# Block products for P4 in layer 0, gate sums moved to POOL and ScalarE, attention read from PSUM

## The chip, the cores and the metric

The kernel runs on one core of a Trainium2 chip. The metric is the device time of one execution in microseconds, taken as the median of several runs. A profiled execution, with every instruction's start and end, is read beside it. The engines are named as in the profile: PE is TensorE's matmul, PEld its weight load, DVE is VectorE, ACT is ScalarE, POOL is GpSimd, and SP is SyncE, which issues most DMAs.

## The reference

128 graphs of 128 nodes with 512 features go through two layers of attention with 8 heads of 64. Everything is float32.

```python
# layer 0, for each graph
Q, K, V = x @ W_q + b_q, x @ W_k + b_k, x @ W_v + b_v
scores = Q K^T / sqrt(64)                       # per head
scores += a[:, None] + c[None, :] + b_g + log(adj + 1e-9)   # a = x @ w_g[:512], c = x @ w_g[512:]
x = softmax(scores) V + x
# layer 1
q, k, v = x @ Wq.T + bq, x @ Wk.T + bk, x @ Wv.T + bv
logits = q k^T / sqrt(64) + log(clip(adj, 1e-8))
out = softmax(logits) v @ Wo.T + bo
x = layer_norm(x + out) * gamma + beta
```

## The kernel before

Four graphs make a tile. There are 64 tiles in a row: tiles 0 to 31 are layer 0 and tiles 32 to 63 are layer 1, and each layer 1 tile reads what the layer 0 tile of the same graphs stored in DRAM (`X1D`). A tile has three matrix products of 512x512 (V, Q, K), and a layer 1 tile a fourth (O), which is taken for the tile before, so that its attention has time to finish. The last tile has its own path.

Each matrix is Strassen-Winograd: seven products of half the size, P1 to P7, instead of eight. A whole product is eight matmuls of 256 columns (sixteen records in the trace) that accumulate in one PSUM bank. Bank `a` (tags p0 and p3, alternating by matrix) takes P1, then P6 and P7 on top of it, each copied out by ACT (t1, u2, u3) before the next is added, and at last P4. Bank `b` (p2) takes P5 and then P3. DVE adds the copies to the banks to get the four output blocks: C11 from P2 and t1, C22 from P5 and u3, C12 from P3 and u2, C21 from bank `a` after P4. A product named in `inside` is itself done by seven products of a quarter of the size ("block products", function `inner` inside `matrix`): four phases, and after each DVE accumulates a block of the bank into t1 (P2) or u3 (P4) and adds parts of it to the output. Before the change `INSIDE` holds P2 for tiles 1 to 63 and P4 for tiles 33 to 63 only; the Q and K of tile 32 and the O of tile 32 have neither. POOL makes the sums of operands: `sums` the four T tiles, `inner_sums` the sums for a block product, and `Strassen.combine_inner` the sums of the weights.

The order is written out by hand. A matrix has seven slots, and the list `row_` says which product goes to which slot (`SLOTS`, and `phases` for the four phases of P2). P4's phases come in slots 0, 2, 3 and 4 of the next matrix. Everything else is put ahead of a slot (`pre`) or behind it (`post`) with `put`, counted from the tile's first slot (`first`) or from the first slot after its K (`a`). `InOrder` makes every engine keep the program's order, so an instruction that waits holds up all that stands behind it on its engine.

Attention of a tile runs while the next tile's matrices are computed. `scores` makes K Q^T of four graphs, in the order of `graphs`: the first, second and fourth go to PSUM buffers of tag s (two of them, two banks each), the third to p1 and the free one of p0 and p3 (`spare`). ACT takes exp from PSUM to SBUF; in layer 0 the gate's c is its bias. `weigh` multiplies by the transposed adjacency on DVE. `mix` multiplies by V, which has a column of ones for the sums, into two more buffers of tag s; ACT copies them to SBUF (`OR`), and `normalise` divides on DVE. In layer 0 it also adds x on POOL and stores the tile. In layer 1 `move` transposes blocks by 16 DMAs for each pair of graphs, and `turn` transposes inside the blocks on DVE.

In layer 0 `gate` multiplies a graph's x by one half of w_g and sums it, in one DVE instruction, eight times in a tile. `add_row` adds the V bias to x on POOL. `count` keeps a record of whether the softmax sums were in range.

Of the kernel before, what the change touches and what calls it, by code (L numbers as in the profile page):

```python
# [134 lines left out]
def fast_path(ctx, tc, args, GOOD, bad):  # L135
# [38 lines left out]
    INSIDE = {t: ("P2", "P4") if t > NG else ("P2",) if t else () for t in range(LAST)}  # L174
# [78 lines left out]
    def gate(t, b, s):  # L253

        if (b, s) == (0, 0):
            C[t] = small.tile([P, 2, G], F32, tag="c", name=f"c_{t}", bufs=2)
        nc.vector.scalar_tensor_tensor(
            GW[:, 2], XN[t, b // 2][:, b % 2], 1.0, GW[:, s], op0=ALU.mult, op1=ALU.mult,
            accum_out=C[t][:, s, b : b + 1],
        )  # L260
# [37 lines left out]
    def matrix(n, name, W, Bs, side, out_tile, dst, bias=None, inside=("P2",)):  # L298
# [60 lines left out]
        def unit(i):  # L359
            i, *phase = i.split(".")  # L360
            if phase:
                if i in inside:
                    return inner(i, *phase)
                if (i, *phase) == ("P2", "1"):
                    t["c"] = bank("p1")
                    product("P2", t["W"], t["B"], t["c"], side, True)
                    add(0, 0, t["c"], t["t1"])
                return
            if i == "P4" and i in inside:
                return  # L370
            if i == "C22":
                return add(1, 1, t["b"], t["u3"])
            if i == "P1":
                t["W"], t["B"] = W(), Bs()
                out_tile()
                t["a"] = bank("p3" if n % 2 else "p0")
            elif i == "P5":
                t["b"] = bank("p2")
            p = t["b" if i in ("P5", "P3") else "a"]
            product(i, t["W"], t["B"], p, side, i in ("P1", "P5"))  # L380
            if i == "P1":
                kept("t1", p, 0, 2)
            elif i == "P6":
                kept("u2", p, None, 1)
            elif i == "P7":
                kept("u3", p, 1, 1)
            elif i == "P4":
                for _, _, o in dst(1, 0, 0, 4):
                    copy(o, p, 1)
            elif i == "P3":  # L390
                if bias is None:
                    add(0, 1, p, t["u2"])
                else:
                    for _, _, o in dst(0, 1, 0, 4):
                        for h, b in biased(0):
                            nc.vector.scalar_tensor_tensor(o[:, h], p[:, h], b, t["u2"][:, h], op0=ALU.add, op1=ALU.add)
# [43 lines left out]
    E = {}  # L440

    def scores(t, graphs, spare=None):
# [4 lines left out]
        for i, b in enumerate(graphs):  # L447
# [20 lines left out]
            if i != 2:  # L468
                pieces = [(e, s[b][2].rearrange("p r c j -> p (r c) j"))]
            for e, p in pieces:  # L470
                nc.scalar.activation(
                    e, p, AF.Exp, scale=SCALE, **({"bias": C[t][:, 1, b : b + 1]} if L == 0 else {})
                )

    def weigh(t, b):
        e = E[t, b]
        nc.vector.tensor_tensor(e, e, AD[t][:, b : b + 1].to_broadcast([P, H, N]), ALU.mult)

    def mix(t, graphs):


        a = {}
        for b in graphs:
            if b % 2 == 0:
                OR[t, b // 2] = work.tile([P, 2, H, HD + 1], F32, tag="o", name=f"o_{t}_{b // 2}", bufs=2)
            a[b] = ps.tile([P, 2, D], F32, tag="s", name=f"av_{t}_{b}", bufs=2)
            for h in range(H):
                for half in HALVES:
                    i = (h % KC) * (HD + 1)
                    nc.tensor.matmul(  # L490
                        a[b][half, h // KC, i : i + HD + 1], E[t, b][:, (h % 2) * KC + h // 2, half], V[t][:, b // 2, h // KC, b % 2 * KC + h % KC],
                        start=True, stop=True,
                    )
        for b, p in a.items():
            nc.scalar.copy(
                OR[t, b // 2][:, b % 2].rearrange("p (s c) d -> p s (c d)", s=2), p[:, :, 0 : KC * (HD + 1)]
            )

    def normalise(t, k):

        L, g = split(t)
        o = OR[t, k]
        if t not in RC:
            RC[t] = small.tile([P, G, 2, KC], F32, tag="rc", name=f"rc_{t}", bufs=2)
        rc = RC[t][:, 2 * k : 2 * k + 2].rearrange("p b s c -> p b (s c)")
        sums_ = o[:, :, :, HD]
        if L == 0:
            ga = GATE[t][:, 2 * k : 2 * k + 2].rearrange("p (b o) -> p b o", o=1).to_broadcast([P, 2, H])
            gated = small.tile([P, 2, H], F32, tag="gated", name=f"gated_{t}_{k}")
            nc.vector.tensor_tensor(gated, sums_, ga, ALU.mult)  # L510
            nc.vector.reciprocal(rc, gated)
            norm = small.tile([P, 2, H], F32, tag="norm", name=f"norm_{t}_{k}")
            nc.vector.tensor_tensor(norm, rc, ga, ALU.mult)
        else:
            nc.vector.reciprocal(rc, sums_)
            norm = rc
        v = o[:, :, :, 0:HD]
        nc.vector.tensor_tensor(
            v, v, norm.rearrange("p b (h o) -> p b h o", o=1).to_broadcast([P, 2, H, HD]), ALU.mult
        )  # L520
        if L == 0:
            xn = XN[t, k]
            for b in range(2):
                xb = xn[:, b].rearrange("p (h d) -> p h d", d=HD)
                nc.gpsimd.tensor_tensor(xb, v[:, b], xb, ALU.add)
            nc.sync.dma_start(X1D[g][2 * k : 2 * k + 2].rearrange("b p d -> p b d"), xn)
# [8 lines left out]
    def move(t, k, engines):  # L535
# [4 lines left out]
        v = OR[t, k].rearrange("p b (c r) d -> p (b c) r d", r=2)  # L540
# [144 lines left out]
    for (which, t), n in at.items():  # L685
        if t < NG:
            phases = EARLY if t == 0 else dict(v=(3, 4, 5, 7), q=(1, 2, 3, 5), k=EARLY)[which]
        elif t == NG or (which, t) == ("v", NG + 1):
            phases = dict(v=(3, 4, 5, 7), q=(1,), k=(0,), o=EARLY)[which]
# [4 lines left out]
        if (which, t) == ("o", NG):  # L694
            phases = (0,)
        for i, slot_ in enumerate(phases):
            row_[7 * n + slot_].append((mats[n], f"P2.{i + 1}"))
        row_[7 * n + 5].append((mats[n], "C22"))

# [9 lines left out]
    for t in range(LAST):  # L709
# [4 lines left out]
        if t + 1 < LAST:  # L714
            visit, weighed, mixed, graphs = (
                (3, (3, 3, 4, 5), (5, 7), (0, 1, 2, 3)), (3, (3, 3, 4, 5), (5, 7), (0, 1, 2, 3)), (5, (5, 5, 5, 7), (7, 9), (2, 3, 0, 1)),
# [4 lines left out]
            for i in range(2):  # L721
                m, k = a + mixed[i], graphs[2 * i] // 2
                put(pre, m, mix, t, (2 * k, 2 * k + 1))
                put(post, m + ((1, 4), (1, 0))[L][i], normalise, t, k)
                if L == 1:
                    put(post, m + (3, 1)[i], move, t, k, [nc.sync, nc.gpsimd] if t == NG and i else [nc.sync])
        if t + 1 < LAST:
            put(post, a + 16, count, t)

        n, late = t + 1, int(t > NG)  # L730
        if n < LAST:
            put(post, first + (2 if t else -1), load_tiles, n)
            for b in range(G):
                put(post, first + (-1 if t == 0 else 2 + (8 if t > NG + 1 else 11) * (b // 2) * late), load_graph, n, b, nc.sync)
                put(post, first + ((8, 9, 16, 16), (19, 20, 23, 24))[late][b], lambda n, b: turn(XT[n][:, b]), n, b)
            put(post, first + (11, 16 if t == NG + 1 else 14)[late], load_adjacency, n, nc.sync)
            put(post, first + (17, 31 if t > NG else 26)[late], turn_adjacency, n)
            put(post, first + (13, 17)[late], lambda n: TS.update({n: quarters(XT[n])}), n)
            put(post, first + (17, 20)[late], lambda n: inner_sums(TS[n], n), n)
            for s in Strassen.SUMS:  # L740
                put(post, first + (18, 24)[late], lambda n, s: sums(TS[n], n, s), n, s)
            if "P4" in INSIDE[n]:
                put(post, first + (18, 24)[late], lambda n: inner_sums(TS[n], n, "P4"), n)
        if L == 0:
            if g + 1 < NG:
                put(post, first + 17, load_natural, t + 1)
            for k, i in enumerate((1, 7, 10, 11, 13, 14, 18, 20)):
                put(post, first + i, gate, t, k // 2, k % 2)
            put(post, first + 21, gate_exp, t)
            for k in range(2):  # L750
                put(post, first + (11, 25)[k], add_row, t, k)
        else:
            put(post, first + (16 if t == NG + 1 else 12), load_natural, t)
            for k in range(2):
                put(post, first + ((27, 28) if t == NG else (28, 29) if t == LAST - 1 else (28, 32))[k], add_row, t, k)
            if n < LAST:
                f = slot("v", n, 0)
                first_pair, turned = (f + 17, f + 18) if t == NG else (f + 15, f + 18)
# [10 lines left out]
                for k in range(2):  # L769
                    put(post, o + (2 + k if t == NG else ((4, 2) if t == LAST - 2 else (4, 5))[k]), residual, t, k)  # L770
                    if t == LAST - 2:
                        continue
                    stat, scaled, end, stored = (((5, 6), 8, 10, 10), ((9, 10), 10, 14, 16))[k]
# [30 lines left out]
    for W, i in (WV, 2), (WQ, 8), (WK, 15):  # L804
        put(post, i, lambda W: Strassen.combine_inner(nc.gpsimd, *W[0], slice(0, 1)), W)
# [11 lines left out]
    def prepare():  # L817
# [4 lines left out]
        RC[t] = small.tile([P, G, 2, KC], F32, tag="rc", name=f"rc_{t}", bufs=2)  # L822

    def normalise_one(b):
        o = OR[t, b // 2][:, b % 2]
        rc = RC[t][:, b].rearrange("p s c -> p (s c)")
        nc.vector.reciprocal(rc, o[:, :, HD])
        nc.vector.tensor_tensor(
            last["o"][:, b].rearrange("p (h d) -> p h d", d=HD), o[:, :, 0:HD],
            rc.rearrange("p (h o) -> p h o", o=1).to_broadcast([P, H, HD]), ALU.mult,  # L830
        )
# [256 lines left out]
```

## Time and profile before

| | |
|---|---|
| median of 3 runs | 3169.83 us (3169.59 to 3171.9) |
| the profiled execution's own time | 3170.23 us |
| its span, from first to last instruction | 3168.5 us |
| granted TensorE clock | 0.999 |
| PE busy | 3149.2 us |
| PEld busy | 2474.2 us |
| DVE busy | 2216.4 us |
| POOL busy | 2116.2 us |
| ACT busy | 1044.1 us |

The busy times overlap, since the engines work side by side. What ends later than it might is told by the chain that ended last and by the waits, not by the busy times. In the rows of groups the numbers behind the bar are the busy time in us, the mean of one instruction in ns, and the engine's idle time ahead of them with what ended it. In the timeline the first number is the start from the beginning of the span and the second the length, both in us.

In the slices of the page POOL is 40% to 50% busy in layer 0, the first 17 or so of 40, and mostly 80% in layer 1.

### The profile page before, as it was taken

The page shows a single profiled execution, that of the slowest core. Times are in us where ns is not written, and L with a number is a line of the kernel's source. Part 1 is how long each engine was busy: PE and PEld are TensorE (multiplying, and loading weights), DVE is VectorE, ACT ScalarE, POOL GpSimd, SP SyncE. Part 2 cuts the span into 40 slices and gives each one's busy share as a digit, 9 for nine tenths or more (in the row PEclk, how much of TensorE's full clock was granted, in tenths as well). Part 3 has the DMA queues.
Part 4 walks back from the last instruction along what each step waited for, and adds up shares of the span by engine and source line. Part 5 has one row for each costly group of instructions (what it writes and reads, how often), then busy time and mean ns, then how long its engine had stood idle before and what let it go on. Part 6 is the DMA issues. An engine that isn't in the chain of part 4 may idle for free.

```text
span 3168.5 us, 98958 instructions
## 1 busy us (share of the span) xinstructions
PE 3149.2 (99%) x41454; PEld 2474.2 (78%) x41454; DVE 2216.4 (70%) x4643; ACT 1044.1 (33%) x1826; POOL 2116.2 (67%) x2337
## 2 busy tenths in 40 slices
PE   9999999999999999999999999999999999999998
PEld 6777777777777777777888888788888888888885
DVE  6677766666766667766677776767676777767676
ACT  2333333333333333333333323323333333233332
POOL 4445544445444445478788888888888888888886
PEclk9999999999999999999999999999999999999999
DMA  5333333333333333343343434343433434343432
GB/s 130 82 81 88 81 80 66 88 81 88 81 72 74 88 82 86 96 102 65 80 91 72 97 73 97 72 101 69 85 84 80 92 71 96 74 99 71 96 67 79
DMA packets 1017264, 266.07 MB, mean 84 GB/s; under 512 B 942704, under 2 KB 949872, under 8 KB 1016816
## 3 DMA queue, kind: packets, MB, share of 16 engines
q1 hardware_dynamic: 1015152, 257.34, 36.6%
q8 instruction: 330, 5.41, 0.7%
q10 hardware_dynamic: 1408, 2.10, 0.2%
q14 instruction: 118, 0.97, 0.1%
q0 software_dynamic: 256, 0.26, 0.1%
HBM read 159.92 MB, written 67.11 MB: 72 GB/s over the span
## 4 chain that ended last, share of the span: by engine, by line
PE 98%; DVE 1%; DMA 0%; POOL 0%; ACT 0%; issue 0%; SPq 0%; POOLq 0%; ACTq 0%; DVEq 0%
PE p3v L132 10%; PE p0q L132 10%; PE p3k L132 10%; PE av L132 7%; PE p2k L132 7%; PE p2q L132 7%; PE p2v L132 7%; PE p0o L132 7%; PE s L132 6%; PE p0v L132 4%; PE p3q L132 4%; PE p0k L132 4%; PE p2o L132 3%; PE p1k L132 3%; PE p1q L132 3%; PE p1v L132 3%
## 5 line engine op out<-in xcount | busy, mean ns | idle before, releaser
L132 POOL TENSOR_TENSOR xn<-o,xn 128x512 f32<-128x512 f32 x128 | 171.9, 1364 | 691.9 <-DVE o L132 691.9
L132 POOL TENSOR_TENSOR xn<-xn,row 128x512 f32<-128x512 f32 x256 | 368.6, 1460 | 24.1 <-DVE gw L132 15.7
L132 DVE TENSOR_TENSOR e<-e,adjT 128x1024 f32<-128x1024 f32 x196 | 272.8, 1406 | 47.2 <-ACT e L132 47.2
L132 DVE SCALAR_TENSOR_TENSOR gw<-xn,gw 128x512 f32<-128x512 f32 x256 | 284.8, 1113 | 1.1
L132 PE MATMUL p3k<-T,wk 128*64 128x256 f32 (+1 forms) x2132 | 250.4, 360 | 0.0
L132 PE MATMUL p3v<-wv,T 128*64 128x256 f32 (+1 forms) x2132 | 241.8, 361 | 0.0
L132 PE MATMUL p0q<-T,wq 128*64 128x256 f32 (+1 forms) x2132 | 240.9, 360 | 0.0
L132 POOL TENSOR_TENSOR h<-h,xn 128x512 f32<-128x512 f32 x124 | 157.1, 1288 | 113.0 <-DVE h L132 113.0
L132 ACT COPY o<-av 128x520 f32<-128x520 f32 x256 | 151.8, 593 | 229.4 <-PE av L132 218.4
L132 POOL TENSOR_TENSOR T<-xT 128x512 f32<-128x512 f32 x128 | 206.7, 1615 | 11.1 <-DVE xT L132 11.1
L132 PEld LDWEIGHTS p3k<-T,wk 128*64 128x64 f32 x2132 | 162.2, 137 | 52.8
L132 PE MATMUL s<-qT,kT 64*128 64x128 f32 x3088 | 200.4, 276 | 0.0
L132 PE MATMUL av<-v,e 128*64 128x65 f32 x6272 | 199.7, 221 | 0.0
L132 PEld LDWEIGHTS s<-qT,kT 64*128 64x128 f32 x3088 | 182.7, 188 | 18.1 <-issue 18.0
L132 PEld LDWEIGHTS av<-v,e 128*64 128x64 f32 x6272 | 196.6, 137 | 0.1
L132 PEld LDWEIGHTS p0q<-T,wq 128*64 128x64 f32 x2132 | 150.3, 137 | 57.0
L132 PEld LDWEIGHTS p3v<-wv,T 128*64 128x64 f32 x2132 | 148.1, 137 | 56.7
L132 DVE TENSOR_TENSOR t1v<-p1v,t1v 128x128 f32<-128x128 f32 x189 | 54.8, 290 | 182.4 <-PE p1v L132 182.3
L132 POOL TENSOR_TENSOR h<-h,gamma 128x512 f32<-128x512 f32 x121 | 154.8, 1279 | 32.7 <-ACT h L132 30.4
L132 DVE STREAM_TRANSPOSE xT<-xT 128x512 f32<-128x512 f32 x252 | 170.0, 694 | 0.5 <-issue 0.5
L132 DVE TENSOR_TENSOR xT<-xT,adjT 128x1024 f32<-128x1024 f32 x60 | 128.1, 2174 | 52.0 <-ACT xT L132 52.0
L132 POOL TENSOR_TENSOR h<-h,beta 128x512 f32<-128x512 f32 x121 | 154.7, 1278 | 9.5
(279 smaller groups left out, 7760.2 us busy)
## 6 DMA issues: line engine op xcount, KB each, us to landing
x1d<-xn SPq DMA_DIRECT2D x64, 512.0 KB, 2.9
xT<-x1d SPq DMA_DIRECT2D x512, 64.0 KB, 2.7
xn<-x1d SPq DMA_DIRECT2D x64, 512.0 KB, 5.0
xT<-in_x_dram SPq DMA_DIRECT2D x496, 64.0 KB, 2.9
xn<-in_x_dram SPq DMA_DIRECT2D x62, 512.0 KB, 4.8
aT<-o SPq DMA_DIRECT2D x984, 32.0 KB, 2.0
out_dram<-h SPq DMA_DIRECT2D x60, 512.0 KB, 4.4
adjT<-in_adj_dram SPq DMA_DIRECT2D x256, 64.0 KB, 3.7
```

The lines of the kernel that those rows point to most:

```text
L132: return lambda *args, **kw: self.tc.keep_in_program_order(f(*args, **kw))
```

## The change

1. **P4 in layer 0.** `INSIDE` now gives P4 to tiles 1 to 31 too, so it is done there by seven block products; `combine_inner` is called for both halves of the layer 0 weights, and `inner_sums` is called for P4. The phases of P2 move to later slots in layer 0. C12 is no longer made directly behind P3 but as a unit of its own in the same slot, behind P4.2 and the phases of P2.
2. **Gate.** The product goes to POOL, into one of two buffers (`GW[:, 2]` and `GW[:, 3]`), and the sum to ACT, as an Identity activation with an accumulator (`gate_sum`).
3. **Attention.** `mix` writes each head at a stride of 128 columns and nothing copies it out: `normalise` reads the sums and the values from PSUM, graph by graph. The exp of the second and fourth graph stays in PSUM, in place, and `weigh` reads it there. Adding x to the layer 0 output and its store become `onto_x`, put some slots later.
4. **Order.** In layer 0 `scores` moves from slot 3 to slot 5, with the graphs in the order 2, 3, 0, 1; the mixes come in slots 8 and 11 in both layers (6 and 9 for tile 32). Moves, turns, sums, residuals, statistics and stores move by some slots.

```diff
-    INSIDE = {t: ("P2", "P4") if t > NG else ("P2",) if t else () for t in range(LAST)}
+    INSIDE = {t: ("P2", "P4") if t and t != NG else ("P2",) if t else () for t in range(LAST)}
...
-        nc.vector.scalar_tensor_tensor(
-            GW[:, 2], XN[t, b // 2][:, b % 2], 1.0, GW[:, s], op0=ALU.mult, op1=ALU.mult,
-            accum_out=C[t][:, s, b : b + 1],
-        )
+        nc.gpsimd.tensor_tensor(GW[:, 2 + s], XN[t, b // 2][:, b % 2], GW[:, s], ALU.mult)
+
+    def gate_sum(t, b, s):
+        o = GW[:, 2 + s]
+        nc.scalar.activation(o, o, AF.Identity, accum_out=C[t][:, s, b : b + 1])
...
+            if i == "C12":
+                p = t["b"]
+                if bias is None:
+                    return add(0, 1, p, t["u2"])
+                for _, _, o in dst(0, 1, 0, 4):
+                    for h, b in biased(0):
+                        nc.vector.scalar_tensor_tensor(o[:, h], p[:, h], b, t["u2"][:, h], op0=ALU.add, op1=ALU.add)
+                return
...
             pieces = [(e[:, :KC], s[b][0]), (e[:, KC:], s[b][1])]
             if i != 2:
                 pieces = [(e, s[b][2].rearrange("p r c j -> p (r c) j"))]
+            IN[t, b] = e
+            if i % 2:
+
+                IN[t, b] = pieces[0][1]
+                pieces = [(IN[t, b], IN[t, b])]
...
-        nc.vector.tensor_tensor(e, e, AD[t][:, b : b + 1].to_broadcast([P, H, N]), ALU.mult)
+        nc.vector.tensor_tensor(e, IN.pop((t, b)), AD[t][:, b : b + 1].to_broadcast([P, H, N]), ALU.mult)
...
-            a[b] = ps.tile([P, 2, D], F32, tag="s", name=f"av_{t}_{b}", bufs=2)
+            a = AV[t, b] = ps.tile([P, H, N], F32, tag="s", name=f"av_{t}_{b}", bufs=2)
...
-        for b, p in a.items():
-            nc.scalar.copy(
-                OR[t, b // 2][:, b % 2].rearrange("p (s c) d -> p s (c d)", s=2), p[:, :, 0 : KC * (HD + 1)]
-            )
...
+    def normalise(t, b, o):
...
+        a = AV.pop((t, b))
+        sums_, v = a[:, :, HD], a[:, :, :HD]
+        o = o.rearrange("p (h d) -> p h d", d=HD)
+        norm = rc.rearrange("p (h o) -> p h o", o=1).to_broadcast([P, H, HD])
+        if split(t)[0] == 0:
+            ga = GATE[t][:, b : b + 1]
+            gated = small.tile([P, H], F32, tag="gated", name=f"gated_{t}_{b}")
+            nc.vector.tensor_scalar(gated, sums_, ga, None, ALU.mult)
             nc.vector.reciprocal(rc, gated)
+            nc.vector.scalar_tensor_tensor(o, v, ga, norm, op0=ALU.mult, op1=ALU.mult)
         else:
             nc.vector.reciprocal(rc, sums_)
+            nc.vector.tensor_tensor(o, v, norm, ALU.mult)
...
+    def onto_x(t, k):
+
+        xn, o = XN[t, k], OR[t, k]
+        for b in range(2):
+            nc.gpsimd.tensor_tensor(xn[:, b], o[:, b], xn[:, b], ALU.add)
+        nc.sync.dma_start(X1D[t][2 * k : 2 * k + 2].rearrange("b p d -> p b d"), xn)
...
         if t < NG:
-            phases = EARLY if t == 0 else dict(v=(3, 4, 5, 7), q=(1, 2, 3, 5), k=EARLY)[which]
+            phases = dict(v=(5, 7, 9, 10), q=(4, 5, 7, 9), k=(3, 4, 5, 7))[which] if t else EARLY
...
         row_[7 * n + 5].append((mats[n], "C22"))
+        row_[7 * n + 9].append((mats[n], "C12"))
...
-                (3, (3, 3, 4, 5), (5, 7), (0, 1, 2, 3)), (3, (3, 3, 4, 5), (5, 7), (0, 1, 2, 3)), (5, (5, 5, 5, 7), (7, 9), (2, 3, 0, 1)),
+                (5, (5, 5, 5, 6), (8, 11), (2, 3, 0, 1)), (3, (3, 3, 4, 5), (6, 9), (0, 1, 2, 3)), (5, (5, 5, 5, 6), (8, 11), (2, 3, 0, 1)),
...
-                put(post, m + ((1, 4), (1, 0))[L][i], normalise, t, k)
-                if L == 1:
-                    put(post, m + (3, 1)[i], move, t, k, [nc.sync, nc.gpsimd] if t == NG and i else [nc.sync])
+                put(post, m + ((0, 0), (0, 0))[L][i], normalise_pair, t, k)
+                if L == 0:
+                    put(post, m + (4, 3)[i], onto_x, t, k)
+                else:
+                    put(post, m + (3, 2)[i], move, t, k, [nc.sync, nc.gpsimd] if t == NG and i else [nc.sync])
...
-            put(post, first + (17, 20)[late], lambda n: inner_sums(TS[n], n), n)
+            put(post, first + (18, 25)[late], lambda n: inner_sums(TS[n], n), n)
             for s in Strassen.SUMS:
-                put(post, first + (18, 24)[late], lambda n, s: sums(TS[n], n, s), n, s)
+                put(post, first + (19, 26)[late], lambda n, s: sums(TS[n], n, s), n, s)
...
-            for k, i in enumerate((1, 7, 10, 11, 13, 14, 18, 20)):
+            for k, i in enumerate((1, 3, 6, 8, 8, 12, 14, 16)):
                 put(post, first + i, gate, t, k // 2, k % 2)
+                put(post, first + (5, 6, 8, 10, 12, 14, 16, 18)[k], gate_sum, t, k // 2, k % 2)
...
-                put(post, first + ((27, 28) if t == NG else (28, 29) if t == LAST - 1 else (28, 32))[k], add_row, t, k)
+                put(post, first + ((27, 28) if t == NG else (27, 28) if t == LAST - 1 else (27, 36))[k], add_row, t, k)
...
-                first_pair, turned = (f + 17, f + 18) if t == NG else (f + 15, f + 18)
+                first_pair, turned = (f + 17, f + 18) if t == NG else (f + 11, f + 18)
...
     for W, i in (WV, 2), (WQ, 8), (WK, 15):
-        put(post, i, lambda W: Strassen.combine_inner(nc.gpsimd, *W[0], slice(0, 1)), W)
+        for k in range(2):
+            put(post, i + 20 * k, lambda W, k: Strassen.combine_inner(nc.gpsimd, *W[0], slice(k, k + 1)), W, k)
```

## The prediction

> **What bounds the kernel now.** I read the page's first part, then the chain that ended last, then the timeline of two tiles.
>
> ```profile
> PE 3149.2 (99%) x41454; PEld 2474.2 (78%) x41454; DVE 2216.4 (70%) x4643; ACT 1044.1 (33%) x1826; POOL 2116.2 (67%) x2337
> ...
> PE 98%; DVE 1%; DMA 0%; POOL 0%; ACT 0%; issue 0%; SPq 0%; POOLq 0%; ACTq 0%; DVEq 0%
> ```
>
> TensorE is the chain. Busy PE alone would prove little, so I added the waits of PE: under 8 us in all, nearly all in the first and last tile. A saving counts only if it shortens TensorE's list or its waits, and there are almost no waits to remove. The windows of one tile of each layer (from one call of `scores` to the next; columns PE, PEld, DVE, ACT, POOL):
>
> ```profile
> 915.11:958.43 43.32, 43.32 (x566) 32.57 (x564) 29.91 (x60) 15.41 (x28) 20.07 (x21) 1.00 0.34 81
> 2247.61:2302.17 54.56, 54.56 (x737) 44.38 (x736) 39.06 (x86) 17.20 (x29) 45.34 (x53) 1.00 0.41 86
> ```
>
> The spacing is 43.32 us for every layer 0 tile and 54.56 for nearly all of layer 1. In layer 1 POOL is the second load, 9 us behind PE. PE's timeline prices the two forms of a block:
>
> ```profile
> 547.47 1.90 PE L132 MATMUL p2q<-T,wq 128*64 128x256 f32 x16
> 549.19 1.90 PE L132 MATMUL p3q<-T,wq 128*64 128x256 f32 x16
> 550.92 0.39 PE L132 MATMUL p1q<-innerP,wq 128*64 128x128 f32 x4
> 551.14 0.39 PE L132 MATMUL p1q<-xT,wq0i 128*64 128x128 f32 x4
> 551.36 1.90 PE L132 MATMUL p0k<-xT,wk 128*64 128x256 f32 x16
> ```
>
> Starts count, not durations (they overlap): a whole product takes 1.727 us, one of seven block products 0.218.
>
> **Part 1: P4 in seven.** Seven blocks are 1.53 us, so a matrix saves 1.727 - 1.529 = 0.198 us on PE. It concerns tiles 1 to 31 (tile 32 is excluded before and after), three matrices each: 93 x 0.198 = **18.4 us**, 0.59 per tile. Pessimistic check: layer 1's tile sums to 54.42 us from these pitches and the layer 0 remainder, and takes 54.56; spread over its 56 blocks that is 0.221 each and 16.7 us saved.
> Per matrix DVE gets three 128x128 accumulations (0.288), two 128x128 adds (0.292) and one 128x256 (0.426): 1.87 us, 5.6 per tile. ACT loses the C21 copies, 0.59 + 4 x 0.47 = 2.5. POOL gets four 128x128 sums, 0.46 each uncontended, 3.7 together at layer 1's rows, and once per weight five small ops (0.5 to 1.0 each). What could stall PE is a step waiting for DVE's accumulation, or P4.1 for ACT's copy of u3. Layer 1 runs this very sequence (P4.1 after the next P1, the others after P3, P6, P5) and shows no such wait; the new layer 0 phases are its phases with the o matrix left out. Cost 0.
>
> **Part 2: the gate.**
>
> ```profile
> L132 DVE SCALAR_TENSOR_TENSOR gw<-xn,gw 128x512 f32<-128x512 f32 x256 | 284.8, 1113 | 1.1
> L132 POOL TENSOR_TENSOR h<-h,gamma 128x512 f32<-128x512 f32 x121 | 154.8, 1279 | 32.7 <-ACT h L132 30.4
> L132 ACT ACTIVATE h<-h,rs 128x512 f32<-128x512 f32 x121 | 92.1, 809 | 21.2 <-POOL rs L132 21.2
> ```
>
> DVE loses 8 x (1.11 + 0.08 accumulator read) = 9.5 us per tile. POOL gains 8 x 1.28 = 10.2. ACT gains 8 sums; no row has an accumulating activation, so between 0.76 (pitch of the last row) and 1.1; I take 0.85, 6.8 us. New wait: ACT's sum waits for POOL's product, and the u and t1 copies that release PE's banks queue behind it; POOL's third product waits for ACT's first sum (two buffers). Products stand two or more slots (2 us each) ahead of most sums. Walking POOL's queue (sums end about 4 us before `scores`, then count, two products, a row add) it is 2 us or more early in a steady tile. The cover goes in tile 0, where weight combination delays the second product: its sum ends near 26.2, t1q near 27.0, and P6 of q is due at 26.1. I take +1 us once.
> Tile sums, layer 0: DVE 29.9 - 9.5 + 5.6 + 0.6 (part 3) = 26.6; ACT 15.4 - 2.5 - 2.4 + 6.8 = 17.3; POOL 20.1 + 10.2 + 1.8 to 3.7 = 32 to 34, against PE's 42.7. None becomes the bound.
>
> **Part 3: attention from PSUM.** Four ACT copies of av (593 ns) go, 2.4 us per tile. DVE's pair 1.23 + 0.25 + 2 x 0.17 becomes two of 0.69 (row v<-p2v,u2v 128x512, 692 ns) + 0.20 + 0.17: +0.6 us a tile, +0.35 in layer 1. The price is that PSUM is held longer. The two s buffers go round: i=0 to A, i=1 to B, i=3 to A, then av to B, A, B, A. With the odd graphs' exp left in PSUM, the first pair's second av (buffer A) waits for DVE's fourth weigh, which was not so before. The change puts that mix one slot later. Is it enough? Layer 1, `scores` at 2247.61:
>
> ```profile
> 2249.57 1.27 POOL L132 TENSOR_TENSOR T<-xT 128x512 f32<-128x512 f32 x1
> 2250.92 2.14 POOL L132 TENSOR_TENSOR T<-xT,T 128x512 f32<-128x512 f32 x1
> 2253.02 2.25 POOL L132 TENSOR_TENSOR T<-xT 128x512 f32<-128x512 f32 x1
> ...
> 2251.84 2.29 DVE L132 TENSOR_TENSOR xT<-xT,adjT 128x1024 f32<-128x1024 f32 x1
> 2254.06 2.29 DVE L132 TENSOR_TENSOR e<-e,adjT 128x1024 f32<-128x1024 f32 x1
> 2256.28 0.28 DVE L132 TENSOR_TENSOR t1o<-p1o,t1o 128x128 f32<-128x128 f32 x1
> 2256.66 0.29 DVE L132 TENSOR_TENSOR h<-p1o,t1o 128x128 f32<-128x128 f32 x1
> 2256.87 0.68 DVE L132 TENSOR_TENSOR h<-p2o,u3o 128x512 f32<-128x512 f32 x1
> ```
>
> A weigh takes 1.22 us alone (layer 0) and 2.29 here, POOL's sums 1.27 and 2.25: they take turns, whoever asked first. [...] PSUM rows bear that out (0.68 beside a running POOL sum), so the second and fourth weighs cost 1.22. Then the second starts at 4.23 after `scores`, the third asks at 5.37, POOL's third sum at 5.41: DVE goes first, the fourth weigh ends near 9.0. PE's list (s 3.77, P7 1.78, P2.1 0.65, P1 1.73, P4.1 0.65, P2.2 0.22, first av 0.93) needs it at 9.73. Cost 0, by 0.7 us. [...] The rows show no such surcharge (0.69 from PSUM and from SBUF at 128x512), so I keep 0, but the margin is 0.04 us. Below nothing is excluded, since PE does not wait there now. In layer 0 POOL's row adds can block one or two weighs: end 8.8 to 9.6, still in time.
> Activation into PSUM has no row; nearest is exp from PSUM to SBUF, 1.06 to 1.12; the sum takes that, a tenth either way.
>
> **Moved steps.** C12 now stands behind P2's adds on DVE; its reader frees the bank for P5, which starts 2.6 us after P3's slot ends, and DVE needs 1.6 for what is queued (0.29 + 0.42 + 0.88): 0. POOL's sums come one slot later in layer 0: behind the last transpose (about 9.5 us before `scores`) T2 is ready at -6.8, and P6 wants it at -3.9: 0. Second mix: DVE divides the first pair within about 2 us, three slots ahead. SP: the x1d stores follow the later `onto_x` and still precede the load of that buffer (slots 14 and 17). In layer 1, 32 transposing DMAs take SP 22.5 us; `move` begins, as now, when P2.4 of o frees aT (2208.3), so 16 end near 2219 and land by 2221.5; the first `turn`, now at slot 11 (about 2224.6), has 3 us. If it failed, DVE and then PE would stand. Later residuals, statistics and stores feed only the output: 0. Last tile: four copies leave a chain that is partly DVE's; -0.5 to -1.5, I take -1.
>
> **Sum:** -18.4 + 1 - 1 = -18.4 against the profiled execution's 3170.23 (span 3168.5): 3151.8. The median of the runs is 0.4 lower: **3151.5 us**.
>
> **Rivals.**
> (B) POOL first in layer 1: 0.47 x 30 = 14 us back, 3165.5; half the tiles, 3158.5. For: a 0.04 us race, the same in every tile. Against: the rows' equal durations.
> (C) Slower: a weigh from PSUM is blocked like one from SBUF, place the same second av. With 2.2 us each for two of them, the fourth ends at 10.9 (layer 1) and 10.7 (layer 0): 1.2 x 30 + 1.0 x 31 = 67 us, 3218. It decides from 1.6 us per weigh in layer 1, and has eaten the whole gain at about 1.8. Against: PSUM rows beside POOL keep 0.68 to 0.69.
> (D) The change doesn't do all it says: blocks of 0.221 us, and ACT held by POOL's products for 0.2 us a tile (31 x 0.2 = 6): 3159.5.
>
> **How the numbers follow.** (A) 0.60, 3148 to 3154; (B) 0.20, half of it below 3163; (C) 0.06; (D) 0.14, mostly below 3163. 0.2% is 6.3 us, about what can be told from no change here: the line is 3163.5. Faster 0.82, same 0.11, slower 0.07. The range takes A with the bounds of head and tail, D, and B up to its full size: 3147 to 3166.
>
> **What would show it.** Tile spacing 42.73 in layer 0 and 54.56 in layer 1; DVE's gw group gone, POOL's there at about 1.3 us; e weighs from s near 1.22. B and C: PE waiting on DVE before av, once per tile. D: PE waiting on ACT's u or t1 copies. A layer 0 spacing at 43.3 or above would make the prediction wrong.

## The result, and the profile after

| | before | after |
|---|---|---|
| median of the runs | 3170.11 us | 3148.77 us (3148.59 to 3149.19) |
| ratio, 95% interval | | 0.9932 [0.9915, 0.9949] |
| span of the profiled execution | 3168.5 us | 3147.1 us |
| layer 0 spacing of `scores` | 43.32 us | 42.73 us |
| layer 1 spacing | 54.56 us | 54.56 us |

The change takes 21.3 us off; the time is 2.7 us below the predicted 3151.5 us and inside the stated range. (The median of before is from four runs here, one more than was shown before the prediction.)

First the page of the changed kernel, its busy times and the chain that ended last:

```profile
PE 3130.4 (99%) x42570; PEld 2506.0 (80%) x42570; DVE 2098.2 (67%) x4941; ACT 985.2 (31%) x1927; POOL 2350.6 (75%) x2732
...
PE 99%; DVE 0%; DMA 0%; POOL 0%; issue 0%; ACT 0%; SPq 0%; DVEq 0%; POOLq 0%
```

TensorE is still the whole chain. It has 1116 more matmul records (42570 against 41454) and is busy 18.8 us less: in 93 matrices 28 records of 128 columns (seven blocks of four) replace 16 of 256 columns, which is 12 records more and seven eighths of the columns. The two stretches from one call of `scores` to the next, tile 20 of layer 0 and tile 47 in layer 1 (columns PE, PEld, DVE, ACT, POOL, granted clock, DMA share, GB/s):

```profile
906.60:949.33 42.73, 42.73 (x602) 33.78 (x601) 27.91 (x66) 15.76 (x35) 29.40 (x33) 1.00 0.35 81
2228.50:2283.06 54.56, 54.56 (x737) 45.09 (x736) 37.88 (x90) 14.94 (x25) 42.66 (x53) 1.00 0.39 83
```

A layer 0 tile became 0.59 us shorter and a layer 1 tile stayed as it was, both with PE busy from end to end. In layer 0 POOL went from 20.07 to 29.40 and DVE from 29.91 to 27.91.

Where the 21.4 us of span went can be told with four anchors: the first `scores`, that of tile 31, that of tile 32, and the last.

| stretch | before | after | difference |
|---|---|---|---|
| start to `scores` of tile 0 | 48.64 | 52.00 | +3.36 |
| tile 0 to tile 31 | 1343.02 | 1324.63 | -18.39 |
| tile 31 to tile 32 | 44.58 | 41.13 | -3.45 |
| tile 32 to the last tile | 1685.79 | 1685.29 | -0.50 |
| last `scores` to the end | 46.43 | 44.03 | -2.40 |

The first and the third row belong together: `scores` now stands two slots later in layer 0, two products of 1.727 us, and at the border to layer 1 it moves back. Without that shift the head is 0.1 us shorter. So there are two real terms: 18.4 us in the 31 gaps of layer 0, and 2.4 us in the last tile.

The groups of the page and of the list by form, for the parts that the change touches (busy us, mean ns | idle time before them):

```profile
L132 POOL TENSOR_TENSOR gw<-xn,gw 128x512 f32<-128x512 f32 x256 | 324.2, 1282 | 97.1 <-ACT gw L132 94.3
L132 ACT ACTIVATE gw<-gw 128x512 f32<-128x512 f32 x256 | 160.9, 630 | 38.9 <-POOL gw L132 38.8
L132 ACT ACTIVATION_READ_ACCUMULATOR gw<-gw 128x1 f32 x256 | 49.7, 194 | 0.0
L132 DVE TENSOR_TENSOR e<-e,adjT 128x1024 f32<-128x1024 f32 x98 | 143.5, 1464 | 65.5 <-ACT e L132 65.5
L132 DVE TENSOR_TENSOR e<-s,adjT 128x1024 f32<-128x1024 f32 x98 | 119.0, 1214 | 0.0
```

DVE's gate group is gone. A gate product on POOL is 1.282 us. A sum on ACT is two instructions of 630 and 194 ns that overlap, 0.72 us from start to end (mean of the 256). The 98 weighs `e<-s` from PSUM take 1.21 us each; those with both sources in SBUF average 1.46, from 1.21 to 2.37. The long ones (24 of the 98, from 1.50 on) all start while a row add or a sum of POOL is running.

The close race of the prediction is the third weigh of a layer 1 tile. DVE's timeline, tile 47, from `scores` at 2228.50 (start, length):

```profile
2230.77 2.02 DVE L132 TENSOR_TENSOR xT<-xT,adjT 128x1024 f32<-128x1024 f32 x1 [1.73 <-ACT xT L132]
2232.71 1.21 DVE L132 TENSOR_TENSOR xT<-s,adjT 128x1024 f32<-128x1024 f32 x1
2233.85 1.21 DVE L132 TENSOR_TENSOR e<-e,adjT 128x1024 f32<-128x1024 f32 x1
...
2236.15 1.22 DVE L132 TENSOR_TENSOR e<-s,adjT 128x1024 f32<-128x1024 f32 x1
```

And POOL's beside it:

```profile
2231.79 2.15 POOL L132 TENSOR_TENSOR T<-xT,T 128x512 f32<-128x512 f32 x1
2233.88 2.31 POOL L132 TENSOR_TENSOR T<-xT 128x512 f32<-128x512 f32 x1
```

The third weigh starts at 2233.85, 0.03 us ahead of POOL's third sum, and keeps its 1.21 us; POOL's sum is the one that is stretched, to 2.31. The fourth weigh ends at 2237.37, 8.87 us after `scores`. The lead is 0.04 to 0.05 us in every tile from 35 to 62, also in tile 48, where both start 0.1 to 0.2 us sooner than in the others: there the first weigh is shorter, and both requests follow its end, DVE's behind the second weigh and POOL's behind the second sum, which the first weigh had held up.

### The profile page after: what moved, and what is told of

Its sections match the earlier page's. It is cut to its first block, busy times and chain, and to the rows that moved or that the text cites. A ratio compares the mean times of both kernels' runs of the same rounds, so it can differ in the third digit from the quotient of the medians.

```text
span 3147.1 us, 102047 instructions
## 1 busy us (share of the span) xinstructions
PE 3130.4 (99%) x42570; PEld 2506.0 (80%) x42570; DVE 2098.2 (67%) x4941; ACT 985.2 (31%) x1927; POOL 2350.6 (75%) x2732
## 4 chain that ended last, share of the span: by engine, by line
PE 99%; DVE 0%; DMA 0%; POOL 0%; issue 0%; ACT 0%; SPq 0%; DVEq 0%; POOLq 0%
PE p3v L132 10%; PE p0q L132 10%; PE p3k L132 10%; PE av L132 8%; PE p2k L132 7%; PE p2v L132 7%; PE p2q L132 7%; PE p0o L132 7%; PE s L132 6%; PE p0v L132 4%; PE p0k L132 4%; PE p3q L132 4%; PE p2o L132 3%; PE p1k L132 3%; PE p1q L132 3%; PE p1v L132 3%
## 5 line engine op out<-in xcount | busy, mean ns | idle before, releaser
L132 POOL TENSOR_TENSOR gw<-xn,gw 128x512 f32<-128x512 f32 x256 | 324.2, 1282 | 97.1 <-ACT gw L132 94.3
L132 POOL TENSOR_TENSOR xn<-xn,row 128x512 f32<-128x512 f32 x256 | 334.4, 1328 | 1.2 <-DMA bq<-in_L_gnn_bq_dram 1.2
L132 POOL TENSOR_TENSOR T<-xT 128x512 f32<-128x512 f32 x128 | 193.4, 1511 | 140.5 <-DVE xT L132 135.8
L132 PE MATMUL p3k<-T,wk 128*64 128x256 f32 (+1 forms) x2068 | 234.7, 350 | 0.0
L132 PE MATMUL p3v<-wv,T 128*64 128x256 f32 (+1 forms) x2068 | 225.9, 351 | 0.0
L132 PE MATMUL p0q<-T,wq 128*64 128x256 f32 (+1 forms) x2068 | 225.1, 350 | 0.0
L132 DVE TENSOR_TENSOR e<-e,adjT 128x1024 f32<-128x1024 f32 x98 | 143.5, 1464 | 65.5 <-ACT e L132 65.5
L132 POOL TENSOR_TENSOR h<-h,gamma 128x512 f32<-128x512 f32 x121 | 154.8, 1279 | 27.9 <-ACT h L132 27.9
L132 ACT ACTIVATE gw<-gw 128x512 f32<-128x512 f32 x256 | 160.9, 630 | 38.9 <-POOL gw L132 38.8
L132 PE MATMUL p0o<-wo,T_o 128*64 128x256 f32 (+1 forms) x1368 | 155.9, 353 | 0.5 <-ACT u3o L132 0.5
L132 PEld LDWEIGHTS p0o<-wo,T_o 128*64 128x64 f32 x1368 | 106.8, 137 | 30.0 <-ACT u3o L132 0.8
```

Source lines behind the costliest of these rows:

```text
L132: return lambda *args, **kw: self.tc.keep_in_program_order(f(*args, **kw))
```

## The experiments

All of them start from the changed kernel, and a run's difference is told against its 3148.77 us.

**e1: the block products alone undone.**

```diff
-    INSIDE = {t: ("P2", "P4") if t and t != NG else ("P2",) if t else () for t in range(LAST)}
+    INSIDE = {t: ("P2", "P4") if t > NG else ("P2",) if t else () for t in range(LAST)}
...
-        for k in range(2):
-            put(post, i + 20 * k, lambda W, k: Strassen.combine_inner(nc.gpsimd, *W[0], slice(k, k + 1)), W, k)
+        put(post, i, lambda W: Strassen.combine_inner(nc.gpsimd, *W[0], slice(0, 1)), W)
```

> The changed kernel with P4 of layer 0 whole again (and the second half of the layer 0 weights' sums left out); gate, attention and the new order stay. Theory: the tiles' gain is the seven block products alone, so layer 0 is spaced 43.32 us again, 31 x 0.592 = 18.4 us come back, and 3148.8 becomes 3167.2; what is left against 3170.1, about 3 us, is the last tile's. Rival: gate, attention and order carry part of the gain, layer 0 stays below 43.3 us and the time below 3162.

Measured: 3168.01 us, ratio to before 0.9992 [0.9983, 1.0001]; layer 0 spacing 43.32, layer 1 54.56. The 31 gaps give back 18.39 us, against 93 x 0.198 = 18.41. Gate and attention, without the block products, are worth about 2 us. The interval of the ratio reaches 1, so that this rests on the spans: the last tile takes 44.62 us from its `scores` to the end, against 46.43 before.

**e2 and e10: the gate on DVE again**, first in the slots of the new product, then in those of the kernel before.

```diff
-        nc.gpsimd.tensor_tensor(GW[:, 2 + s], XN[t, b // 2][:, b % 2], GW[:, s], ALU.mult)
+        nc.vector.scalar_tensor_tensor(
+            GW[:, 2], XN[t, b // 2][:, b % 2], 1.0, GW[:, s], op0=ALU.mult, op1=ALU.mult,
+            accum_out=C[t][:, s, b : b + 1],
+        )
...
-                put(post, first + (5, 6, 8, 10, 12, 14, 16, 18)[k], gate_sum, t, k // 2, k % 2)
```

> The changed kernel with the gate as before, product and sum in one DVE instruction, in the changed kernel's slots. Theory: DVE has 42.7 - 26 = 16 us to spare in a layer 0 tile and takes the 9.5 us back without PE waiting: 42.73 us spacing, 3148 to 3151. Rival: an instruction of 0.7 to 1.7 us between the accumulations makes PE wait for DVE, at least 0.2 us in each tile, spacing 42.9 or more, 3155 or more; then the gate's move is what lets P4 be done in blocks.

Measured: 3167.85 us, ratio to before 0.999 [0.9981, 0.9999]; layer 0 spacing 43.28. My own expectation was wrong and the rival's right: with the block products in place, the gate on DVE costs 0.55 us in each layer 0 tile, 17.9 us over the 31 gaps. DVE's timeline of tile 20 in e2 shows where, 13 us after `scores` (918.42):

```profile
931.49 0.68 DVE L132 SCALAR_TENSOR_TENSOR gw<-xn,gw 128x512 f32<-128x512 f32 x1
932.10 0.08 DVE L132 DVE_READ_ACCUMULATOR gw<-xn,gw 128x1 f32 x1
932.22 0.69 DVE L132 SCALAR_TENSOR_TENSOR gw<-xn,gw 128x512 f32<-128x512 f32 x1
932.83 0.08 DVE L132 DVE_READ_ACCUMULATOR gw<-xn,gw 128x1 f32 x1
932.83 0.29 DVE L132 TENSOR_TENSOR u3v<-p3v,u3v 128x128 f32<-128x128 f32 x1
933.04 0.28 DVE L132 TENSOR_TENSOR t1v<-p1v,t1v 128x128 f32<-128x128 f32 x1
933.35 0.29 DVE L132 TENSOR_TENSOR v<-p1v,t1v 128x128 f32<-128x128 f32 x1
```

and PE's beside it:

```profile
931.25 1.90 PE L132 MATMUL p0q<-T,wq 128*64 128x256 f32 x16
933.27 0.44 PE L132 MATMUL p3v<-wv,T 128*64 128x128 f32 x4
933.70 0.44 PE L132 MATMUL p1v<-wv,innerP 128*64 128x128 f32 x4
933.97 0.39 PE L132 MATMUL p1v<-wv0i,xT 128*64 128x128 f32 x4
```

The whole product p0q started at 931.25 and needs 1.73 us, so the next block p3v was due at 932.98. It starts at 933.27, because DVE's accumulation of that bank (u3v) ends only at 933.12: two gates stood ahead of it. The block after it, due 0.22 us later, starts 0.43 later: DVE reads its bank p1v twice, for t1v and then for v, and is done at 933.64. The view of waits lists three waits for u3v in the whole run, 1.1 us in all; stalls of 0.2 to 0.3 us show only in PE's pitch, the time from one start to the next.

> The gate is again one VectorE instruction per half, as in e2, but in the slots of the kernel before (1, 7, 10, 11, 13, 14, 18, 20) instead of the product's new ones. In e2 two of them stood in front of the accumulation that releases the bank for P4.4 of v, and layer 0 tiles took 43.28 us. Theory (it is the place in VectorE's queue that costs, not the 9.5 us of work): at other slots that stall at 14.6 us after scores goes, and what is left is at most another, smaller one; spacing 42.73 to 42.95, total 3149 to 3157. Rival (the block products of three matrices leave VectorE's queue no place where 1.1 us of gate is free): some accumulation is late at the old slots too, spacing 43.2 or more, 3164 to 3180.

Measured: 3166.33 us, ratio 0.9986 [0.9979, 0.9993]; layer 0 spacing 43.20. The rival again: at the old slots the stall at 14.6 us is gone, and another of the same kind has come at 24.5 to 27 us, in the matrix q. DVE's timeline of e10, tile 20 (`scores` at 917.35):

```profile
941.86 1.19 DVE L132 SCALAR_TENSOR_TENSOR gw<-xn,gw 128x512 f32<-128x512 f32 x1
942.99 0.08 DVE L132 DVE_READ_ACCUMULATOR gw<-xn,gw 128x1 f32 x1
942.99 0.28 DVE L132 TENSOR_TENSOR u3q<-p0q,u3q 128x128 f32<-128x128 f32 x1
943.30 0.29 DVE L132 TENSOR_TENSOR qT<-p0q,u3q 128x128 f32<-128x128 f32 x1
943.51 0.28 DVE L132 TENSOR_TENSOR t1q<-p1q,t1q 128x128 f32<-128x128 f32 x1
943.82 0.29 DVE L132 TENSOR_TENSOR qT<-p1q,t1q 128x128 f32<-128x128 f32 x1
```

PE's block of the bank p1q was due 0.22 us after the one at 943.78:

```profile
944.17 0.44 PE L132 MATMUL p1q<-innerP,wq 128*64 128x128 f32 x4
```

The accumulation u3q waits 1.1 us behind a gate that takes 1.19 instead of 0.68, and PE waits until the add of qT from p1q, three instructions further on, ends at 944.11. In the changed kernel the same accumulation finds DVE idle for 0.46 us. Two placements were tried, and no others; that none would do is not shown.

**e3 and e7: exp to SBUF**, in all tiles and in the last tile alone.

```diff
-            if i % 2:
+            if False:                     # e3
+            if i % 2 and t < LAST - 1:    # e7
```

> The changed kernel with every exp written to SBUF, so that no weigh reads PSUM. Theory [...]: in layer 1 the second and third weigh take 2.3 us again, DVE's first accumulation of P2 ends 8.95 us after scores instead of about 6.8, PE wants it at 8.58 for P2.2 and waits 0.4 us in each of 29 or 30 tiles; the spacing goes from 54.56 to about 55.0, the time from 3148.8 to 3161 or 3162, plus 1 us in the last tile. Layer 0 stays at 42.73 or loses up to 0.2 us a tile. Rival: PSUM reads save DVE time that nobody waits for, spacing and time stay (3149 to 3150).

Measured: 3175.21 us, ratio 1.0014 [1.0007, 1.0021]; layer 1 spacing 55.40, layer 0 unchanged at 42.73. The place was right and the size too small, 0.84 us a tile instead of 0.4. Two lines of e3, tile 47, from DVE and from PE (`scores` at 2239.40):

```profile
2245.70 2.29 DVE L132 TENSOR_TENSOR e<-e,adjT 128x1024 f32<-128x1024 f32 x1
```

```profile
2248.63 0.44 PE L132 MATMUL p1o<-woi,innerP_o 128*64 128x128 f32 x4 [0.47 <-DVE h L132]
```

The third weigh is blocked by POOL too and ends 2.0 us later after `scores` than in the changed kernel. As expected, what waits first is the block P2.2 of o, which needs the bank p1o: DVE reads it for t1o and then for h right behind this weigh, and PE starts the block 9.23 us after `scores` instead of 8.59. So two weighs from PSUM per layer 1 tile save 0.84 us that the old way of weighing would cost in this order.

> The changed kernel with every exp written to SBUF in the last tile only. Theory: of the 2.4 us by which the end from the last scores to the span's end became shorter, 1.0 us is the second weigh that no longer takes its turn with POOL's row adds (PE's wait for h goes from 0.30 back to 1.3 us); the rest is the ACT copies. Spans of 3148.1 instead of 3147.1. Rival: the end is bound by DVE's last instructions, and nothing changes.

Measured: 3150.46 us, ratio 0.9935 [0.9919, 0.9952]; span +1.4 us, where 1.0 was expected. PE's wait for h in the last tile is back:

```profile
3109.77 0.44 PE L132 MATMUL p1o<-wo,innerP_o 128*64 128x128 f32 x4 [1.35 <-DVE h L132]
```

From the last `scores` to the end it takes 45.65 us, against 44.03 in the changed kernel and 46.43 before: 1.6 of the last tile's 2.4 us come from the exp in PSUM.

**e4 and e9: a delay ahead of the third weigh**, one idle memset or five, in tiles 33 to 62.

```diff
         e = E[t, b]
+        if t > NG and b == 0 and t < LAST - 1:
+            for _ in range(5):            # e4: once
+                nc.vector.memset(idle, 1.0)
```

> The changed kernel with one idle memset of 128x64 (about 0.1 us) on DVE ahead of the third weigh in layer 1, tiles 33 to 62. Theory: [...] the third weigh asks at 5.48 after scores instead of 5.38, POOL's third sum at 5.43 wins, the weigh takes 2.3 us instead of 1.2, the fourth ends at 10.1 to 10.2 instead of 8.9, the second av wants it at 9.73, and PE waits 0.4 to 0.5 us per tile: 30 tiles, 3148.8 to about 3161 to 3164. Rival: DVE's order has 0.8 us to spare there and 0.1 us is swallowed: 3148.8.

Measured: 3148.78 us, spacing 54.56, nothing changed; the expectation was wrong. The memset overlaps the end of the second weigh, the third moved by only 0.06 us, and it still kept its short length. Yet its recorded start is now 0.02 to 0.04 us behind that of POOL's third sum in every tile from 35 to 62, and it is still POOL's sum that is stretched (2.32 us, against 1.16 for the weigh). So 0.06 us don't lose the race, and the recorded starts don't tell who wins it at this distance.

> Five idle memsets of 128x64 on VectorE ahead of the third weigh in tiles 33 to 62, where one moved its request by 0.06 us and changed nothing; five should move it by 0.35 to 0.5 us, well behind the start of GpSimd's third sum. The output is unchanged. Theory [...]: GpSimd's third sum runs alone, 1.27 us instead of 2.3, the third weigh is blocked and recorded at about 2.0 to 2.3 us instead of 1.2, ends near 8.0 instead of 6.6, and the fourth near 10.2; the second av, due at 9.73, waits 0.4 to 0.5 us in each of 30 tiles: layer 1 spacing about 55.0, in all 3161 to 3164. Rival (VectorE goes first whenever both ask within the length of a GpSimd sum[...]): the third weigh keeps about 1.2 us, the fourth ends at 9.4, still before 9.73: spacing 54.56, 3149.

Measured: 3165.43 us, ratio 0.9984 [0.9976, 0.9991]; layer 1 spacing 55.1 (from 54.56). DVE, POOL and PE of e9, tile 47 (`scores` at 2236.60):

```profile
2242.04 0.88 DVE L132 MEMSET idle<- 128x64 f32 x5
2242.83 1.56 DVE L132 TENSOR_TENSOR e<-e,adjT 128x1024 f32<-128x1024 f32 x1
```

```profile
2242.04 1.27 POOL L132 TENSOR_TENSOR T<-xT 128x512 f32<-128x512 f32 x1
2243.27 2.26 POOL L132 TENSOR_TENSOR T<-T,xT 128x512 f32<-128x512 f32 x1
```

```profile
2246.85 1.15 PE L132 MATMUL av<-v,xT 128*64 128x65 f32 x32 [0.34 <-DVE e L132]
```

Now POOL's third sum is first and takes 1.27 us alone; the weigh ends at 2244.39, 1.08 us after POOL is done; the second av waits. This is rival B of the prediction as it was described, 0.54 us a tile, 16.7 us in all (the prediction said 0.47 and 14). The delay came out longer than the 0.35 to 0.5 us expected: the third weigh starts 6.23 us after `scores` instead of 5.35, 0.8 behind POOL's third sum. By this shift alone the fourth weigh would have ended at about 9.75 us, against the 9.73 at which the second av is due, and it ends at 10.11; so most of the wait comes from POOL's going first. By estimate this would cost the same without the delay, since in both runs the weigh's end hangs on POOL's end and not on its own start: in the kernel before, the third weigh of tile 47 starts 1.2 us ahead of the end of POOL's sum (2254.06 and 2255.27, in the prediction's lines), in e9 0.5 us, and both end 1.08 us after it. So the rival was real, and the order that keeps it away holds with a margin of over 0.06 and under 0.9 us.

**e5: the first mix one slot earlier**, in both layers. Each of the two rows is edited in the same way:

```diff
-                (5, (5, 5, 5, 6), (8, 11), (2, 3, 0, 1)),
+                (5, (5, 5, 5, 6), (7, 11), (2, 3, 0, 1)),
```

> The changed kernel with the first mix one slot earlier (7 instead of 8) in tiles 0 to 31 and 33 to 62. Theory: the second av needs the buffer that the fourth weigh reads; it would start 7.13 us after scores, the weigh ends at 8.8 to 9.2 in both layers, so PE waits 1.6 to 2.1 us in each of 61 tiles: spacing 44.4 to 44.8 and 56.4, in all about 108 us, 3257. Rival: the hold of the PSUM buffers is not what the later slot is for, and the time stays at 3149.

Measured: 3293.43 us, ratio 1.0385 [1.0368, 1.0402]. PE's waits (us in total, times, longest) name the fourth weigh:

```profile
PE av L132 <- DVE e L132: 115.3, 62, 2.1
```

Layer 1 is as expected, +1.93 us a tile. Layer 0 lost more than the 1.7 to 2.1 us expected, for two reasons. In most tiles the fourth weigh ends at 9.2 us, the late end of what I took, and the second av starts 0.13 us behind it (+2.25 us a tile); and in some tiles there is more. PE in such a tile:

```profile
1014.03 1.10 PE L132 MATMUL av<-v,e 128*64 128x65 f32 x32
1017.16 1.15 PE L132 MATMUL av<-v,e 128*64 128x65 f32 x32 [2.03 <-DVE e L132]
1018.12 3.61 PE L132 MATMUL p3q<-xT,wq 128*64 128x256 f32 x16
1021.46 0.71 PE L132 MATMUL p0v<-wv,T 128*64 128x128 f32 x8
```

and the windows of the same stretch, whose seventh column is the granted clock:

```profile
1014.00:1018.10 4.10, 2.07 (x68) 1.96 (x66) 3.60 (x6) 1.41 (x5) 2.50 (x2) 1.00 0.00 0
1018.10:1019.70 1.60, 1.60 (x16) 1.11 (x13) 0.00 (x0) 0.00 (x0) 0.00 (x0) 0.53 0.00 0
1019.70:1021.40 1.70, 1.70 (x10) 1.16 (x8) 0.00 (x0) 0.00 (x0) 0.00 (x0) 0.50 0.00 0
1021.40:1024.00 2.60, 2.60 (x34) 2.21 (x32) 1.34 (x6) 1.45 (x4) 0.71 (x1) 0.96 0.00 0
```

After a wait of 2.03 us the clock falls to a half for 3.4 us, and one whole product takes 3.34 us instead of 1.73. That happens in 11 of the 32 layer 0 tiles. Such a tile takes 46.66 us instead of 44.98, and the eleven together cost 18.6 us.

**e8: av copied out by ACT**, sums and values in two copies, and divided from SBUF.

```diff
-        sums_, v = a[:, :, HD], a[:, :, :HD]
         o = o.rearrange("p (h d) -> p h d", d=HD)
+        sums_, v = small.tile([P, H], F32, tag="sums", name=f"sums_{t}_{b}"), o
+        nc.scalar.copy(sums_, a[:, :, HD])
+        nc.scalar.copy(o, a[:, :, :HD])
```

> The changed kernel with av copied out of PSUM by ACT again (values and sums as two copies) and divided from SBUF. Theory: no PE wait in either layer, spacings stay at 42.73 and 54.56, since the buffers come free earlier and DVE has time; only the last tile pays, up to 1 us: 3149 to 3150. Rival: ACT, which also does the gate's sums, gets late with its copies of u and t1, or DVE's division takes turns with POOL again and is late for an accumulation, 0.2 us or more a tile: 3155 or more.

Measured: 3205.63 us, ratio 1.0109 [1.0092, 1.0125]; layer 0 spacing 43.19, layer 1 55.75. I had expected no cost, and it is 57 us. In layer 1 nearly all of it lies at the second av of the first mix (1.15 of 1.19 us). ACT, then PE (tile 45, `scores` at 2152.46):

```profile
2162.42 0.17 ACT L132 COPY sums<-av 128x8 f32<-128x8 f32 x1 [1.22 <-PE av L132]
2162.71 0.58 ACT L132 COPY o<-av 128x512 f32<-128x512 f32 x1
```

```profile
2161.26 1.10 PE L132 MATMUL av<-v,xT 128*64 128x65 f32 x32
2163.35 1.15 PE L132 MATMUL av<-v,xT 128*64 128x65 f32 x32 [0.98 <-ACT o L132]
```

The second av starts 0.06 us after ACT's copy of the first. The program of e8 says why: in 29 of the 30 tiles 33 to 62 both av of the first mix are given the same PSUM buffer (in tile 45 both lie from bank 6 on), while in the changed kernel the two lie in different ones (banks 6 and 4). So the 1.19 us are the price of this choice of buffers; what the copies cost in layer 1 with two buffers e8 does not tell. In layer 0 the buffers alternate as in the changed kernel. There DVE divides from SBUF and takes 1.43 us instead of 0.75 for the second graph in tile 20 (the 128 divisions of layer 0 average 1.135 us, against 0.751 from PSUM in the changed kernel), so the accumulations of q behind it are late as in e10.

**e6: block products and order alone**: the edits of e2, e3 and e8 together.

> The changed kernel with only the block products and the new order left: gate on DVE, every exp to SBUF, av copied out by ACT (values and sums as two copies) and divided there. Theory: layer 1 loses the 0.4 us a tile of the run with every exp in SBUF (12 to 13 us), layer 0 loses more than that run since DVE has 36 us or more of work in 42.7 and the gate's instructions collide with POOL's: 0.2 to 0.6 us a tile, 6 to 18 us; 3168 to 3180, so the block products alone would have gained nothing. Rival: the gain is the block products' whatever the rest does: 3150 to 3155.

Measured: 3219.81 us, ratio 1.0154 [1.0137, 1.0171]; layer 0 spacing 43.93, layer 1 55.40. That is 49 us slower than before, far from the 3168 to 3180 expected. In layer 0 the stalls of e2 (matrix v) and of e8 (matrix q) come together, 1.20 us a tile. In layer 1 the two av lie in different buffers here, and the spacing is that of e3. The block products in this order, with nothing done for DVE, are a loss. An order made for them alone was not tried, nor the old single copy of each av.

## Why the prediction came out right, point by point

**What bounds.** Right: TensorE's list is the time, and the saving is what leaves that list. The sum holds too, but for its last digit: 3151.8 less 0.4 is 3151.4.

**Part 1, the blocks.** The term of 18.4 us is right: 18.39 in the gaps, and 18.39 returned by e1. The pessimistic 0.221 per block, which had made 16.7, is out. That no PE step would wait for an accumulation holds for the changed kernel as a whole. The reason given for it, that layer 1 runs this sequence without such a wait, is too weak: it would have said the same of e2, where PE does wait. The cost of 0 came true because the gate left DVE in the same change, which the prediction did not see as its condition; to that extent it was luck.

**Part 2, the gate.** POOL's 1.28 us is right. The tile sums were rough, but none became the bound, as said: DVE 27.9 us (26.6 predicted), ACT 15.8 (17.3), POOL 29.4 (32 to 34). ACT's sum was taken too long, 0.85 us against 0.72. Two things matter more. The first is a mis-sized term: the +1 us in tile 0 did not come. ACT's lines of the head:

```profile
24.32 0.63 ACT L132 ACTIVATE gw<-gw 128x512 f32<-128x512 f32 x1 [3.81 <-POOL gw L132]
24.86 0.19 ACT L132 ACTIVATION_READ_ACCUMULATOR gw<-gw 128x1 f32 x1
24.95 0.82 ACT L132 ACTIVATE t1q<-p3q,bq 128x256 f32<-128x256 f32 x2
```

ACT does wait 3.81 us for POOL's second product, with t1q queued behind it, as described; but the sum ends at 25.05, not near 26.2, and t1q at 25.77, 0.23 us before P6 of q starts (26.00). The walk of POOL's queue was about 1.2 us too long there.

The second is a reading. The prediction treated the gate as a move that costs nothing and brings nothing, from the tile sums: 26.6 us of DVE against 42.7 of PE. With the gate still on DVE the sum would have been some 36 (26.6 + 9.5); in tile 20 of e2 it is 33.1, also far below PE, and yet e2 and e10 lose 16 to 18 us of the 18.4. A sum of busy time does not price an engine that stands between two steps of PE; the place in its queue does. Undone singly, the block products (e1) and the gate (e2) each leave 2 to 3 us of the 21: in this order neither carries the gain by itself.

**Part 3, attention.** What the prediction read from its PSUM rows (0.68 us beside a running POOL sum) is that a read from PSUM doesn't wait for POOL, and for the weighs that came true: from PSUM they took 1.21 to 1.22 us, all 128 of them, and one from SBUF in tile 47 took 2.02 beside POOL's 2.15. In e9, where POOL asks 0.8 us sooner, its sum takes 1.27 us and the weigh ends after it. A PSUM source costs a weigh nothing extra, as the prediction had it: in the four lines of tile 47 it is 1.21 us from PSUM and 1.21 from SBUF. Rival B, which could win or lose by 0.04 us in the prediction, was further off: in e4 the third weigh is 0.06 us later and nothing changes. The margin was wider than the 0.04 us in the recorded starts. The fourth weigh ended at 8.87 us, near 9.0 as worked out, and in layer 0 at 8.8 or 9.25 (tiles 18 to 21), within 8.8 to 9.6. Exp into PSUM cost about the same as exp into SBUF, 1.093 and 1.114 us at 128x1024 in layer 0.
The tail was mis-sized: 2.4 us instead of 1. The prediction counted the missing copies, not that the last weighs also go from PSUM. PE of before, in the last tile:

```profile
3128.89 0.44 PE L132 MATMUL p1o<-wo,innerP_o 128*64 128x128 f32 x4 [1.33 <-DVE h L132]
```

and after:

```profile
3108.89 0.44 PE L132 MATMUL p1o<-wo,innerP_o 128*64 128x128 f32 x4 [0.30 <-DVE h L132]
```

This wait alone is 1.03 us shorter, and e7 brings it back (1.35). The head (-0.1 us instead of +1), the tail and the 0.5 us of layer 1 are the whole difference between 18.4 predicted and 21.3.

**Moved steps.** Zero, as said: PE has no wait that it did not have before, but for one of 0.2 us. One of the moved places, the slot of the first mix, is sized by e5; the others were not tried one by one.

**The rivals.** B is a real mechanism with the size given, and did not happen (e9). C is out: no weigh from PSUM took over 1.22 us. D's two terms are both zero: 18.39 us is what blocks of 0.218 us give, and PE waits for ACT twice in the whole run, 0.7 us in all, as before.

## What to carry to other kernels

A step that seems to bring nothing by itself can be what makes another one pay: try each part undone from the finished change, since e1 and e2 leave 2 to 3 us of 21. Look at what else such a run changes: in e8 the buffers moved, and most of its loss is theirs. Where an engine releases the bottleneck's buffers in order, ask what stands in its queue ahead of each release, not how busy it is. A mean pitch of the bottleneck per tile finds stalls of 0.2 us that the view of waits leaves out.

## What the runs showed of the hardware that was not expected

**The clock after a wait.** In e5 the granted clock fell to 0.50 to 0.53 after PE had waited 2.03 us. By the starts of the two matmuls around the wait, a gap of 2.23 to 2.34 us was followed by half speed in 11 of 28 tiles, and a gap of 1.82 to 1.97 us in none of 34. The eleven stretches of half clock ahead of the last tile are 3.413 us long each, and their starts lie whole multiples of 3.413 us apart (27, 40 or 53). The same step is in the clock records of the kernels before and after: their one stretch at full clock is 3153.915 and 3133.435 us long, 924 and 918 times 3.4133, and so they differ by six steps, 20.480 us. With e5's trace divided into steps of this length from the start of such a stretch, it can be told which tiles are hit: every gap with 2.08 us or more inside one step was followed by the fall (11 of 11), and no gap with 2.00 us or less was (0 of 51). That is not so everywhere in the program: in the head of e5 a gap of 2.22 us lay wholly inside one step, and the clock stayed. In layer 0 of e5 a wait that was followed by the fall cost 1.7 us more than itself (46.66 us a tile against 44.98).

**POOL or DVE first.** Two requests recorded 0.04 to 0.05 us apart were decided for DVE in every tile from 35 to 62, and in e4 also with DVE recorded 0.02 to 0.04 us behind POOL. The starts in a profile of POOL and DVE don't settle an order at that distance; 0.8 us (e9) do.
